# A scatter without waits among its own kind, a table cleared from DRAM, and loads issued earlier, in a two-layer graph network

## The chip, the core and the metric

The kernel runs on one core of one Trainium2 chip. A core has a matrix engine (PE, whose weight loads are listed apart as PEld), a vector engine (DVE), an activation engine (ACT), a general engine (POOL), a sequencer (SP) that here only issues transfers, and 16 DMA engines that all queues share. The metric is the device time of one execution in microseconds; the median of three runs is given. A profile is one further execution with the hardware profiler on; its span is the time from the first to the last instruction.

## What is computed

The input is x of 6250 nodes with 256 features and 100 000 edges, sorted by destination. Four layers follow each other, and each adds its result to x:

```python
x = x + gat(layernorm(x), edge_index, ...)      # 8 heads x 32, softmax over the edges of a node, relu
x = x + moe_top1(layernorm(x), ...)             # 32 experts, 256 -> 64 -> 256, relu
x = x + rgcn(layernorm(x), edge_weight, ...)    # 16 relations, weighted sum over edges
x = x + moe_top2(layernorm(x), ...)             # 8 experts, 256 -> 512 -> 256, gelu, layernorm
```

The first mixture of experts is the one that the change bears on:

```python
logits = xf @ router_w.T + router_b
idx = jnp.argmax(logits, axis=-1)
w1t = jnp.take(W1, idx, axis=0)
h = jnp.einsum('nd,ndh->nh', xf, w1t) + jnp.take(b1, idx, axis=0)
h = jax.nn.relu(h)
w2t = jnp.take(W2, idx, axis=0)
out = jnp.einsum('nh,nhd->nd', h, w2t) + jnp.take(b2, idx, axis=0)
out = jax.nn.relu(out)
```

So every node goes through one of 32 small networks, and the kernel sorts the nodes by expert so that a tile of 128 nodes needs one expert's weights.

## The kernel before

**Attention.** After a preparation (L224 to L312) and a pass over the nodes that writes a row of 272 floats for each to the DRAM table H_tab and the destinations' terms to ad_tab (L651), a loop of 98 rounds (L1117) takes 1024 edges each. A round's eight gathers (L444, POOL) fetch 128 rows of 1088 B each by index. PE forms sums by destination (L502, L518), and L557 picks each edge's destination term from `aw`, a small tile that `load_terms` (L476) reads from ad_tab over SP's queue two rounds ahead, into one of three buffers. `load_dst` reads destination numbers on ACT's queue, also two rounds ahead, into `db` with two buffers.

**Order.** The whole loop stands under `tc.manual_schedule()` (L1108): every engine executes its instructions in the order in which the Python code emits them. In each round, between the picks of one group and the sums of another, `fill` (L1134) emits some of the following layer's work, by fixed budgets of time for each kind.

**The second layer beside it.** Nodes are handled in three chunks of tiles of 128 nodes, (0,6), (6,22) and (22,49), so that a chunk can start when the attention sums of its nodes are done. For each chunk generators emit: `take` (residual and norm), `route` (expert of each node, count, slot in the sorted order), `experts`, and `products` (the 16 relation products of the third layer, written to T_tab). `route` ends with a loop over the chunk's tiles (L868): rows are loaded from x1_tab into `xs2`, which has four buffers, three tiles ahead (L859), and scattered to their slots of the DRAM table `x_sort` by an indirect DMA on POOL (L870). The three chunks share one x_sort. Each scatter writes the whole table as far as the tracking of dependences knows, so each waits for the one before it. `experts` then loads tiles of x_sort (`xs`, L928) and of the weight table `w_tab` (L922) on SP, transposes (L915), multiplies (L904, L892), adds into `ys` (L894, two buffers) and stores to y_sort (L935).

**The tables.** Slots of a chunk are padded to whole tiles for each expert, so unused slots have to hold zeros, and w_tab has padding as well. Once, in the first rounds, the generator `flow.consts` (L674) is stepped by `next(boot, None)` (L1133), one step a round. It clears w_tab whole from a tile of zeros in SBUF (L692), fills its parts (L694 to L697), and clears x_sort by 58 DMAs of one tile (L700), four in a round; then the relation weights `wr` are loaded (L705), two a round. `route` waits with its scatters (in the emission of code) until `self.ready` says that the clears are emitted.

**Afterwards.** A second block (L1145) emits what is left of the second layer. Then the third layer gathers rows of T_tab (L444 again, 784 gathers named `ts`), and the last layer follows (L1210 to L1345).

Of the kernel before, what the change touches and what calls it, by code (L numbers as in the profile page):

```python
# [14 lines left out]
ALU = mybir.AluOpType  # L15
AX = mybir.AxisListType
DVE = mybir.EngineType.DVE
SP = mybir.EngineType.SP
# [28 lines left out]
def gnn_ffn_kernel(  # L47
# [91 lines left out]
    ew_sb = const.tile([P, T, NG], F32, name="ew_sb")  # L139
    dst_f = const.tile([P, T, NG], F32, name="dst_f")  # L140

# [20 lines left out]
    B1C = W2C + D  # L162
    w_tab = dram.tile([E1, P, B1C + 4], F32, name="w_tab")
    x1_tab = dram.tile([N, 2 * D], F32, name="x1_tab")
    x2_tab = dram.tile([N, D], F32, name="x2_tab")

    class Chunk:


        def __init__(self, a, b, x_sort=None):  # L170
            self.a, self.b, self.nt = a, b, b - a
            self.xt = (min(N, b * P) - a * P + E1 * (P - 1)) // P
            self.x_sort, self.sorted, self.free, self.taken = x_sort, False, lambda: True, []
            if x_sort is None:
                self.x_sort = dram.tile([self.xt * P, 2 * D], F32, name=f"x_sort{a}_{b}")
            self.y_sort = dram.tile([self.xt * P, D], F32, name=f"y_sort{a}_{b}")

# [46 lines left out]
    with tc.tile_pool(name="prep", bufs=1) as prep, tc.tile_pool(name="prep_p", bufs=1, space=PSUM) as prep_p:  # L224
# [71 lines left out]
        nc.vector.scalar_tensor_tensor(i1f, nat["src"], float(NREL), nat["rel"], op0=ALU.mult, op1=ALU.add)  # L296
        for a, o in ((dgf, dst_f), (srf, src_i), (i1f, idx1), (nat["ew"], ew_sb)):
            for h in range(2):
                w = T // 2
                pt = prep_p.tile([P, w, NG], F32, name="pt", bufs=2)  # L300
                for t in range(w):
                    c = (h * w + t) * P
                    nc.tensor.transpose(pt[:, t, :], a[:, c : c + P], ident[:NG, :NG])
                if a is dgf:
                    nc.vector.tensor_tensor(
                        rlm[:, h * w : (h + 1) * w, :].rearrange("p (q u) g -> p q u g", u=QT),
                        pt.rearrange("p (q u) g -> p q u g", u=QT),
                        lo4[:, h * Q // 2 : (h + 1) * Q // 2, None, :].to_broadcast([P, Q // 2, QT, NG]), ALU.subtract)
                if h == 0:
# [94 lines left out]
    class Group:  # L404


        def __init__(self, pool, g, dynamic):
            self.g, self.pool, self.dynamic = g, pool, dynamic
            if not dynamic:
                self.idx0 = lambda t: src_i[:, t, g : g + 1]  # L410
                self.idx1 = lambda t: idx1[:, t, g : g + 1]
                self.w, self.rl = ew_sb[:, :, g], rlm[:, :, g]
                self.win = lambda i: win[:, i, g : g + 1]
                return
            ii = pool.tile([P, 2, T], I32, name="d_ii")
            fw = pool.tile([P, 2, T], F32, name="d_fw")
            for o, a in ((ii[:, 0], src_i), (ii[:, 1], idx1), (fw[:, 0], dst_f), (fw[:, 1], ew_sb)):
                nc.vector.tensor_copy(o.rearrange("p (t o) -> p t o", o=1), a[:, :, ds(g, 1)])
            self.di = pool.tile([P, T], I32, name="d_di")
            nc.vector.tensor_copy(self.di, fw[:, 0, :])  # L420
# [38 lines left out]
        def load_dst(self):  # L459

            n = GE if self.dynamic else QT * P
            self.db = self.pool.tile([P, n], I32, name="db", bufs=1 if self.dynamic else 2)
            if self.dynamic:
                nc.sync.dma_start(self.db, dst_rows[ds(self.g, 1), :].to_broadcast([P, GE]))
                return
            for q in range(Q):
                nc.scalar.dma_start(self.db[q * QW : (q + 1) * QW, :],
                                    bass.AP(tensor=dst.tensor, offset=dst.offset + self.g * GE + q * n,
                                            ap=[[0, QW], [1, n]]))
# [184 lines left out]
    class Flow:  # L654


        def __init__(self, es, bufs, psum_bufs):

            self.open, self.bufs = 0, 1
            self.ready = False  # L660
            enter = lambda name, **kw: es.enter_context(tc.tile_pool(name=name, **kw))
# [11 lines left out]

        def consts(self, zero):  # L674

# [15 lines left out]
            nc.vector.tensor_copy(self.rwT, pr[:, : KC * E1].rearrange("p (k e) -> p k e", k=KC))  # L691
            nc.sync.dma_start(w_tab.rearrange("e p w -> p e w"), zr[:, None, : B1C + 4].to_broadcast([P, E1, B1C + 4]))  # L692
            for k in range(KC):
                nc.sync.dma_start(w_tab[:, :, k * H1 : (k + 1) * H1], f1_w1[:, k * P : (k + 1) * P, :])  # L694
            nc.sync.dma_start(w_tab[:, :H1, W2C:B1C], f1_w2)
            nc.sync.dma_start(w_tab[:, H1, W2C:B1C], f1_b2)
            nc.sync.dma_start(w_tab[:, :H1, B1C], f1_b1)  # L697
            yield
            for c in range(zero.shape[0] // P):
                nc.sync.dma_start(zero[c * P : (c + 1) * P, :], zr)  # L700
                if c % 4 == 3:
                    yield
            self.ready = True
            for r in range(NREL):
                nc.sync.dma_start(self.wr[:, :, r, :], rel_w[r].rearrange("(k p) o -> p k o", p=P))  # L705
                if r % 2 == 1:
                    yield

# [49 lines left out]
        def route(self, ck):  # L758
# [93 lines left out]
            nc.vector.tensor_reduce(cnt, le, AX.X, ALU.add)  # L852
            while not (ck.free() and self.ready):
                yield None
# [13 lines left out]
            for j in range(ck.nt):  # L868
                r, xs2 = ahead.pop(0)
                nc.gpsimd.indirect_dma_start(  # L870
                    out=ck.x_sort[:, :], out_offset=bass.IndirectOffsetOnAxis(ap=ck.slot[:r, j : j + 1], axis=0),
                    in_=xs2[:r, :], in_offset=None)
                if j + 3 < ck.nt:
                    ahead.append(rows(j + 3))
                if j % 8 == 7:
                    yield 0, 0.1

        def experts(self, ck):
# [7 lines left out]
            for s in range(np_ + 5):  # L886
                if 4 <= s < np_ + 4:
# [3 lines left out]
                    for j in range(n):  # L891
                        nc.tensor.matmul(po[:, j * D : (j + 1) * D], lhsT=hid[:, j, :], rhs=lv["w"][j][: H1 + 1, W2C:B1C], start=True, stop=True)  # L892
                    ys = pool.tile([P, 2, D], F32, name="ys", bufs=2)
                    nc.vector.scalar_tensor_tensor(ys[:, :n, :], po[:, : n * D].rearrange("p (n d) -> p n d", n=n), 0.0,  # L894
# [23 lines left out]
                if 2 <= s < np_ + 2:  # L918
                    lv = live[s - 2]
                    for j in range(lv["n"]):  # L920
                        w = pool.tile([P, B1C + 4], F32, name="w", bufs=6)
                        nc.sync.dma_start(w, w_tab[ds(lv["e"][j], 1)].rearrange("o p w -> (o p) w"))  # L922
                        lv["w"].append(w)
                if s < np_:
                    c, n = pairs[s]
                    lv = live[s] = {"c": c, "n": n, "e": [], "w": []}
                    xs = lv["xs"] = pool.tile([P, 2, 2 * D], F32, name="xs", bufs=5)
                    nc.sync.dma_start(xs[:, :n, :], xs_rows[:, c : c + n, :])  # L928
                    for j in range(n):
# [119 lines left out]
    with ExitStack() as es_flow:  # L1049
# [5 lines left out]
        pi = es.enter_context(tc.tile_pool(name="ge_i", bufs=1, space=PSUM))  # L1055
        aws = [pr1.tile([P, Q, 2 * HEADS], F32, name=f"aw{i}") for i in range(3)]
        for a in aws:
# [113 lines left out]
    with tc.If(flag(2) > 0):  # L1171
# [3 lines left out]
        with ExitStack() as es_flow:  # L1175
            flow = Flow(es_flow, 1, 2)
            for _ in flow.consts(whole.x_sort):
                pass
# [199 lines left out]
```

## Time and profile before

| | us |
|---|---|
| runs | 3815.41, 3823.86, 3828.49 |
| median | 3823.86 |
| profiled execution | 3459.76 |
| its span | 3458.0 |
| PE busy | 2423.5 (70%) |
| POOL busy | 1713.0 (50%) |
| DVE busy | 1069.1 (31%) |
| ACT busy | 803.6 (23%) |

The profiled execution is 364 us shorter than the median of the runs. The mean granted clock of PE was 0.727 of full speed.

How to read the lines that follow. The page cuts the span into 40 equal slices of 86 us, and a digit gives an engine's busy tenths in a slice, 9 for 90% and more. A group of instructions is a line of code, an engine, an operation and its output and input, with the number of instructions, the busy time and the mean in ns of one, and after the bar the idle time ahead of them and what ended most of it. A line of waits gives an engine, what it was to do, whom it waited for, and the total us, the number of waits and the longest one. A line of the timeline begins with start and duration in us; the bracket at its end has the idle time ahead of the instruction and what released it. A line of a DMA queue gives packets, MB, and the share of the 16 engines' time that they took.

### The profile page before, as it was taken

Reading aid. Unit: us, or ns where it says so; the run is one execution under the profiler, and the core shown is the slowest. Engines: PE = TensorE matmul, PEld = TensorE weight load, DVE = VectorE, ACT = ScalarE, POOL = GpSimd, SP = SyncE. Lnnn points to the kernel's source line nnn. Section 1 sums busy time; section 2 is a strip of 40 time slices with the busy share of each in tenths; the row PEclk is TensorE's granted clock in tenths of the full one; section 3 lists DMA queues with packets and bytes.
Section 4 is the critical chain, followed back from the end, with each engine's and each line's share of the span. In section 5 each row is a group of like instructions: output and inputs, shape, how many; then the busy total and the mean of one; then the engine's idle time right before and its main releaser. Section 6 shows DMA issues by size and latency. Waiting matters only on the chain. (4 is left out here: it accounts for less than half of the span.)

```text
span 3458.0 us, 32167 instructions
## 1 busy us (share of the span) xinstructions
PE 2423.5 (70%) x8917; PEld 1186.0 (34%) x8918; DVE 1069.1 (31%) x2879; ACT 803.6 (23%) x1684; POOL 1713.0 (50%) x1736
## 2 busy tenths in 40 slices
PE   5334457791675987188999966666666666689997
PEld 4212235341453443054444421111111111166665
DVE  7324646562555653011000002121121211242222
ACT  2112223440333443033333310000000000012332
POOL 0447676774757771200000047777777777622222
PEclk9655576885676999589999975555555555569999
DMA  4697687675886774586444453333333333310000
GB/s 146 193 217 244 186 278 229 200 227 177 265 264 186 227 219 161 169 264 219 168 171 170 159 188 105 105 105 105 105 105 105 105 105 105 89 28 19 19 19 20
DMA packets 326688, 533.40 MB, mean 154 GB/s; under 512 B 84966, under 2 KB 182564, under 8 KB 326496
## 3 DMA queue, kind: packets, MB, share of 16 engines
q1 hardware_dynamic: 218060, 277.92, 24.4%
q0 software_dynamic: 83152, 233.62, 23.7%
q10 hardware_dynamic: 25284, 19.67, 1.9%
q8 instruction: 75, 1.23, 0.2%
q14 instruction: 117, 0.96, 0.1%
HBM read 342.80 MB, written 192.42 MB: 155 GB/s over the span
## 5 line engine op out<-in xcount | busy, mean ns | idle before, releaser
L444 POOL DMA_INDIRECT hs<-H_tab,src_i x784 | 765.7, 977 | 428.3 <-issue 212.0
L444 POOL DMA_INDIRECT ts<-T_tab,idx x784 | 743.7, 949 | 330.4 <-issue 238.5
L998 PE MATMUL pb<-wr,xTt 128*128 128x512 f32 (+1 forms) x1568 | 722.2, 617 | 18.6 <-ACT tr L1001 14.1
L502 PE MATMUL qagg<-ts,oh 128*32 128x256 f32 x1568 | 504.6, 630 | 327.7 <-DMA ts<-T_tab,idx 324.0
L998 PEld LDWEIGHTS pb<-wr,xTt 128*128 128x128 f32 (+1 forms) x1568 | 303.9, 198 | 387.8 <-issue 356.7
L502 PEld LDWEIGHTS qagg<-ts,oh 128*32 128x32 f32 x1568 | 90.2, 139 | 719.9 <-DMA ts<-T_tab,idx 640.4
L1001 ACT COPY tr<-pb 128x512 f32<-128x512 f32 (+1 forms) x392 | 228.4, 587 | 452.7 <-PE pb L998 344.1
L509 ACT COPY qs<-qagg 128x264 f32<-128x264 f32 (+1 forms) x196 | 73.9, 377 | 1117.0 <-PE qagg L502 1095.3
L454 DVE TENSOR_TENSOR oh<-iota,rlm 128x256 f32<-128x256 f32 x196 | 83.1, 425 | 799.2 <-PE qagg L502 793.5
L518 PE MATMUL agg<-qs,pl 128*128 128x264 f32 (+1 forms) x392 | 204.4, 619 | 146.2 <-DVE pl L511 81.9
L557 PE MATMUL pe<-aw,oT 128*128 128x64 f32 x392 | 86.4, 362 | 296.2 <-issue 140.0
L952 POOL DMA_INDIRECT yg<-y_sort,slot x49 | 47.1, 961 | 489.0 <-ACT xl L717 291.6
L579 DVE TENSOR_TENSOR hs<-hs,pe 128x2048 f32<-128x2048 f32 x98 | 223.2, 2277 | 0.0
L557 PEld LDWEIGHTS pe<-aw,oT 128*128 128x128 f32 x392 | 76.5, 267 | 339.6 <-issue 247.9
L1328 PE MATMUL ph<-xT,we 128*128 128x512 f32 (+1 forms) x416 | 177.4, 584 | 15.1 <-DMA we<-in_L_ffn_W_dram,ix 11.7
L518 PEld LDWEIGHTS agg<-qs,pl 128*128 128x128 f32 x392 | 91.2, 280 | 270.5 <-ACT qs L509 162.6
L1336 PE MATMUL po<-we,hid 128*128 128x256 f32 (+1 forms) x784 | 171.9, 379 | 0.5 <-DVE we L1314 0.3
L1336 PEld LDWEIGHTS po<-we,hid 128*128 128x128 f32 (+1 forms) x784 | 148.4, 190 | 26.8 <-issue 5.7
L502 PE MATMUL qagg<-hs,oh 128*32 128x264 f32 x1568 | 155.7, 533 | 0.0
L894 DVE SCALAR_TENSOR_TENSOR ys<-pb,xs 128x512 f32<-128x512 f32 (+1 forms) x72 | 49.2, 684 | 324.8 <-PE pb L892 180.0
L904 PE MATMUL pb<-xTe,w 128*64 128x128 f32 x568 | 99.6, 326 | 40.1 <-DMA w<-w_tab 35.3
L915 PE MATMUL pt<-ident,xs 128*128 128x128 f32 x284 | 58.7, 341 | 95.6 <-DMA xs<-x_sort 92.7
(278 smaller groups left out, 2303.7 us busy)
## 6 DMA issues: line engine op xcount, KB each, us to landing
T_tab<-tr SPq DMA_DIRECT2D x384, 256.0 KB
xs<-x_sort SPq DMA_DIRECT2D x70, 512.0 KB
w<-w_tab SPq DMA_DIRECT2D x142, 194.0 KB
y_sort<-ys SPq DMA_DIRECT2D x70, 256.0 KB
x_sort<-xs SPq DMA_DIRECT2D x58, 256.0 KB
db<-in_dst_dram ACTq DMA_DIRECT2D x392, 32.0 KB
hs<-H_tab,src_i POOLq DMA_INDIRECT x784
ts<-T_tab,idx POOLq DMA_INDIRECT x784
```

The source lines that it names most:

```text
L444: nc.gpsimd.indirect_dma_start(out=hs[:, t, :], out_offset=None, in_=table, in_offset=bass.IndirectOffsetOnAxis(ap=idx(t), axis=0))
L454: nc.vector.tensor_tensor(oh, iota[:, None, :n].to_broadcast([P, T, n]), column(self.rl), ALU.is_equal)
L502: nc.tensor.matmul(ps[q * QW : (q + 1) * QW, :width], lhsT=oh[:, t, :], rhs=vals[:, t, :width], start=u == 0, stop=u == QT - 1)
L509: nc.scalar.copy(qs, ps[:, :width])
L518: nc.tensor.matmul(ps[:, :width], lhsT=pl, rhs=qs, start=True, stop=True)
L557: nc.tensor.matmul(pq[:, u * w : (u + 1) * w], lhsT=oT[:, u, :], rhs=aw.rearrange("p q h -> p (q h)"), start=True, stop=True)
L579: nc.vector.tensor_tensor(hv, hv, pv.to_broadcast([P, T, HEADS, HD]), ALU.mult)
L904: nc.tensor.matmul(ph[:H1, j * P : (j + 1) * P], lhsT=lv["w"][j][:, k * H1 : (k + 1) * H1], rhs=xT[:, k, j * P : (j + 1) * P], start=k == ...
L998: nc.tensor.matmul(pr[:r, :], lhsT=xT[:, k, j * P : j * P + r], rhs=self.wr[:, k, q0 : q0 + 2, :], start=k == 0, stop=k == KC - 1)
L1001: nc.scalar.copy(o2, pr[:r, :])
L1328: nc.tensor.matmul(ph[:, :nn], lhsT=we1[:, i, k, c * P : (c + 1) * P], rhs=xT[:, k, :nn], start=k == 0, stop=k == KC - 1)
L1336: nc.tensor.matmul(po[:r, :], lhsT=hid[:, i, c, j * P : j * P + r], rhs=we2[:, i, c, :], start=i + c == 0, stop=i + c == NFC)
```

## The change

The scatters of one chunk are declared independent of each other, and the load of the sorted rows waits for all of them. x_sort is cleared two tiles at a time, one such DMA in a round, from a DRAM table of zeros, z_tab. w_tab has rows of 385 instead of 388 floats, is no longer cleared whole, and its parts are filled one in a round; only its padding is written with zeros. Scatters may be emitted as soon as the clears of as many tiles as the chunk needs have been emitted (`first` is the smallest of these numbers). Destination terms are loaded four rounds ahead into six buffers, destination numbers three rounds ahead into three. POOL is no longer among the engines whose order is that of the code: the scheduler orders it. `ys` has a third buffer. The copy dst_f, which only a fallback path read, is gone.

```diff
-    w_tab = dram.tile([E1, P, B1C + 4], F32, name="w_tab")
+    w_tab = dram.tile([E1, P, B1C + 1], F32, name="w_tab")
+    z_tab = dram.tile([P, 2 * D], F32, name="z_tab")
...
-            self.db = self.pool.tile([P, n], I32, name="db", bufs=1 if self.dynamic else 2)
+            self.db = self.pool.tile([P, n], I32, name="db", bufs=1 if self.dynamic else 3)
...
-        def consts(self, zero):
+        def consts(self, zero, first):
+            nt = zero.shape[0] // P
+
+            def clear(n):
+                n = min(n, nt - self.cleared)
+                if n:
+                    o = zero[self.cleared * P : (self.cleared + n) * P, :].rearrange("(c p) d -> c p d", p=P)
+                    nc.sync.dma_start(o, z_tab[None, :, :].to_broadcast([n, P, 2 * D]))
+                    self.cleared += n
...
-            nc.sync.dma_start(w_tab.rearrange("e p w -> p e w"), zr[:, None, : B1C + 4].to_broadcast([P, E1, B1C + 4]))
-            for k in range(KC):
-                nc.sync.dma_start(w_tab[:, :, k * H1 : (k + 1) * H1], f1_w1[:, k * P : (k + 1) * P, :])
-            nc.sync.dma_start(w_tab[:, :H1, W2C:B1C], f1_w2)
-            nc.sync.dma_start(w_tab[:, H1, W2C:B1C], f1_b2)
-            nc.sync.dma_start(w_tab[:, :H1, B1C], f1_b1)
-            yield
-            for c in range(zero.shape[0] // P):
-                nc.sync.dma_start(zero[c * P : (c + 1) * P, :], zr)
-                if c % 4 == 3:
-                    yield
-            self.ready = True
+            nc.sync.dma_start(z_tab, zr)
+            parts = [(w_tab[:, :, k * H1 : (k + 1) * H1], f1_w1[:, k * P : (k + 1) * P, :]) for k in range(KC)]
+            parts.append((w_tab[:, H1:, W2C:], z_tab[None, H1:, : D + 1].to_broadcast([E1, P - H1, D + 1])))
+            parts.append((w_tab[:, :H1, W2C:B1C], f1_w2))
+            parts.append((w_tab[:, H1, W2C:B1C], f1_b2))
+            parts.append((w_tab[:, :H1, B1C], f1_b1))
+            while self.cleared < first:
+                if parts:
+                    nc.sync.dma_start(*parts.pop(0))
+                clear(2)
+                yield
+            for o, i in parts:
+                nc.sync.dma_start(o, i)
             for r in range(NREL):
                 nc.sync.dma_start(self.wr[:, :, r, :], rel_w[r].rearrange("(k p) o -> p k o", p=P))
-                if r % 2 == 1:
-                    yield
+                clear(2)
+                yield
+            while self.cleared < nt:
+                clear(2)
+                yield
...
-            while not (ck.free() and self.ready):
+            while not (ck.free() and self.cleared >= ck.xt):
                 yield None
...
-                nc.gpsimd.indirect_dma_start(
+                ins = nc.gpsimd.indirect_dma_start(
                     out=ck.x_sort[:, :], out_offset=bass.IndirectOffsetOnAxis(ap=ck.slot[:r, j : j + 1], axis=0),
                     in_=xs2[:r, :], in_offset=None)
+
+                ck.put.append(ins.ins)
+                tc.declare_no_dep(ins.ins, group=ck.key, reason="no two nodes share a slot")
+                tc.add_to_no_dep_group(ck.key, ins.ins)
...
-                    ys = pool.tile([P, 2, D], F32, name="ys", bufs=2)
+                    ys = pool.tile([P, 2, D], F32, name="ys", bufs=3)
...
-                    nc.sync.dma_start(xs[:, :n, :], xs_rows[:, c : c + n, :])
+                    ins = nc.sync.dma_start(xs[:, :n, :], xs_rows[:, c : c + n, :])
+                    for put in ck.put:
+                        tc.add_manual_dep(ins.ins, put.name, mybir.DependencyInfo(
+                            mybir.DependencyClass.Sync, mybir.DependencyReason.DATA), reason="all rows are there")
...
-        aws = [pr1.tile([P, Q, 2 * HEADS], F32, name=f"aw{i}") for i in range(3)]
+        aws = [pr1.tile([P, Q, 2 * HEADS], F32, name=f"aw{i}") for i in range(6)]
...
-        with tc.manual_schedule():
-
-            boot = flow.consts(chunks[0].x_sort)
+        with tc.manual_schedule(engines={PE, DVE, ACT, SP}):
+
+            boot = flow.consts(chunks[0].x_sort, min(ck.xt for ck in chunks))
             groups = [Group(pg, g, False) for g in range(NG)]
-            for g in range(2):
-                groups[g].load_dst()
-                groups[g].load_terms(aws[g % 3])
+            for g in range(4):
+                if g < 3:
+                    groups[g].load_dst()
+                groups[g].load_terms(aws[g])
...
-                if g + 2 < NG:
-                    groups[g + 2].load_dst()
-                    groups[g + 2].load_terms(aws[(g + 2) % 3])
+                if g + 3 < NG:
+                    groups[g + 3].load_dst()
+                if g + 4 < NG:
+                    groups[g + 4].load_terms(aws[(g + 4) % 6])
...
-        with tc.manual_schedule():
+        with tc.manual_schedule(engines={PE, DVE, ACT, SP}):
             while takes or routes or runs or tails:
                 fill(4.0, 8.0, (1, 1, 1, 9))
```

More of the change, by code (lines that the diff above doesn't have):

```diff
@@ L16 @@
 AX = mybir.AxisListType
+PE = mybir.EngineType.PE
 DVE = mybir.EngineType.DVE
@@ L139, in gnn_ffn_kernel @@
     ew_sb = const.tile([P, T, NG], F32, name="ew_sb")
-    dst_f = const.tile([P, T, NG], F32, name="dst_f")
     rlm = const.tile([P, T, NG], F32, name="rlm")
@@ L175, in __init__ @@
                 self.x_sort = dram.tile([self.xt * P, 2 * D], F32, name=f"x_sort{a}_{b}")
+            self.key, self.put = f"put{a}_{b}", []
             self.y_sort = dram.tile([self.xt * P, D], F32, name=f"y_sort{a}_{b}")
@@ L296, in gnn_ffn_kernel @@
         nc.vector.scalar_tensor_tensor(i1f, nat["src"], float(NREL), nat["rel"], op0=ALU.mult, op1=ALU.add)
-        for a, o in ((dgf, dst_f), (srf, src_i), (i1f, idx1), (nat["ew"], ew_sb)):
+        for a, o in ((dgf, None), (srf, src_i), (i1f, idx1), (nat["ew"], ew_sb)):
             for h in range(2):
@@ L308, in gnn_ffn_kernel @@
                         lo4[:, h * Q // 2 : (h + 1) * Q // 2, None, :].to_broadcast([P, Q // 2, QT, NG]), ALU.subtract)
+                if o is None:
+                    continue
                 if h == 0:
@@ L416, in __init__ @@
             fw = pool.tile([P, 2, T], F32, name="d_fw")
-            for o, a in ((ii[:, 0], src_i), (ii[:, 1], idx1), (fw[:, 0], dst_f), (fw[:, 1], ew_sb)):
+            for o, a in ((ii[:, 0], src_i), (ii[:, 1], idx1), (fw[:, 1], ew_sb)):
                 nc.vector.tensor_copy(o.rearrange("p (t o) -> p t o", o=1), a[:, :, ds(g, 1)])
             self.di = pool.tile([P, T], I32, name="d_di")
-            nc.vector.tensor_copy(self.di, fw[:, 0, :])
+            nc.sync.dma_start(self.di, dst_rows[ds(g, 1), :].rearrange("g (t p) -> p (g t)", p=P))
+            nc.vector.tensor_copy(fw[:, 0, :], self.di)
             self.base = pool.tile([P, 1], F32, name="d_base")
@@ L659, in __init__ @@
             self.open, self.bufs = 0, 1
-            self.ready = False
+            self.cleared = 0
             enter = lambda name, **kw: es.enter_context(tc.tile_pool(name=name, **kw))
@@ L920, in experts @@
                     for j in range(lv["n"]):
-                        w = pool.tile([P, B1C + 4], F32, name="w", bufs=6)
+                        w = pool.tile([P, B1C + 1], F32, name="w", bufs=6)
                         nc.sync.dma_start(w, w_tab[ds(lv["e"][j], 1)].rearrange("o p w -> (o p) w"))
@@ L1176, in gnn_ffn_kernel @@
             flow = Flow(es_flow, 1, 2)
-            for _ in flow.consts(whole.x_sort):
+            for _ in flow.consts(whole.x_sort, whole.xt):
                 pass
```

## The prediction, made before the changed kernel had run

> **What bounds the kernel now.** I read the slices of the span first, then the waits, then the timeline at every POOL gap. The slices give busy tenths of 86 us each:
>
> ```profile
> PE   5334457791675987188999966666666666689997
> POOL 0447676774757771200000047777777777622222
> DMA  4697687675886774586444453333333333310000
> ```
>
> To slice 15 POOL's gathers of attention rows set the pace, 784 of them:
>
> ```profile
> L444 POOL DMA_INDIRECT hs<-H_tab,src_i x784 | 765.7, 977 | 428.3 <-issue 212.0
> q1 hardware_dynamic: 218060, 277.92, 24.4%
> x_sort<-xs SPq DMA_DIRECT2D x58, 256.0 KB
> ```
>
> A gather takes 0.98 us and 0.27 us of issue, so 1.25 us; an undisturbed round of eight takes 10.0 us (98 rounds, 114 to 1293 us). Then come routing and scatters of the last chunk (to 1454), its experts (1608), products (1990, PE), relational gathers (3100, POOL), the last FFN (3458, PE). The change touches 114 to 1608 only, so a shift there moves the end by as much. The waits (engine, line, releaser: total us, times, longest) that it aims at:
>
> ```profile
> POOL x_sort L870 <- DMA x_sort<-xs,slot: 102.1, 41, 3.7
> PE pt L915 <- DMA xs<-x_sort: 92.7, 2, 69.2
> PE pe L557 <- DMA aw<-ad_tab: 80.7, 7, 44.4
> DVE ys L894 <- DMA y_sort<-ys: 78.8, 14, 9.8
> ```
>
> The timeline places them (start, us, engine, line; in brackets the wait):
>
> ```profile
> 199.83 8.11 SPq L476 DMA_DIRECT2D aw<-ad_tab  x4
> 209.54 1.09 PE L557 MATMUL pe<-aw,oT 128*128 128x64 f32 x4 [44.44 <-DMA aw<-ad_tab]
> 212.93 1.01 POOL L444 DMA_INDIRECT hs<-H_tab,src_i  x1 [35.11 <-PE qagg L502]
> ...
> 416.34 1.00 POOL L870 DMA_INDIRECT x_sort<-xs,slot  x1 [0.30 <-issue]
> 439.35 1.09 PE L915 MATMUL pt<-ident,xs 128*128 128x128 f32 x4 [23.56 <-DMA xs<-x_sort]
> ...
> 785.92 0.99 POOL L870 DMA_INDIRECT x_sort<-xs,slot  x1 [0.30 <-DVE hs L579]
> 847.20 0.96 POOL L870 DMA_INDIRECT x_sort<-xs,slot  x1 [2.02 <-DMA x_sort<-xs,slot]
> 887.11 1.06 PE L915 MATMUL pt<-ident,xs 128*128 128x128 f32 x4
> ...
> 1358.23 0.99 POOL L870 DMA_INDIRECT x_sort<-xs,slot  x1 [39.15 <-DVE le L850]
> 1450.38 1.56 POOL L870 DMA_INDIRECT x_sort<-xs,slot  x1 [3.50 <-issue]
> ```
>
> Read there: destination terms queued behind the table clears stop PE for 44 us and POOL for 35; six scatters of chunk 1 precede its first experts matmul at 439.35; 16 scatters of chunk 2 hold POOL from 785.9 to 848.5; 27 scatters of chunk 3 run while PE, the weight loads and almost everything else stand still.
>
> **What the Trainium skill says.** "DMA: Bandwidth & Descriptors" has three things. Its section "Why a DMA increments its semaphore by 16 and not by 1" says that a DMA is spread over the largest number of engines, at most 16, that divides the slowest dimension of both patterns, and the rules for authors there warn that a leading broadcast of c copies confines the DMA to c engines. No DMA of the trace before shows this at such a size. "Specifications" puts one engine at some 27 GiB/s (29 GB/s); the trace has 22.9: in 162 to 174 us the hardware queue moved 2.71 MB in 61.7% of 16 engines × 12 us. "Anatomy of one DMA" has about 2 us of fixed completion latency; the trace agrees, with 2.0 us of wait after each 0.96 us scatter.
>
> **The change part by part.**
>
> *Clears.* Before, 58 clears of 256 KB left SBUF with 128 partitions outermost. Now 29 clears of 512 KB go from DRAM to DRAM, and the pattern in the program is 2 × 4 × 16384: its outermost size is the two copies. By the rule each uses two engines, 262,144 B on each. At the trace's 22.9 GB/s that is 11.5 us; at the page's 29, an estimate, 9.0. The descriptors are larger than the trace's, so I take the middle, 10.3. One clear is issued in a round, and a round's gathers also put 8 × 8 × 1088 B = 69.6 KB on each engine, 3.0 us at 23.3 GB/s (software queue, same window). 13.3 us don't fit in 10.0: in the clearing rounds two engines become the bound, and the gathers, whose rows lie on all 16, wait for these two.
>
> When does chunk 1 start? SP issues 24 or 25 clears before the rows of its scatters, and the first scatters wait for the clears' completions. Work on the two engines from 156 us (the first clear): 25 × 10.3 = 257; gathers to group 28, behind which POOL's new order puts the scatters (232 instead of 208 gathers; some 39 are done), 193 × 0.374 = 72; weight table 36 (30 us before, 183 to 213, and a sixth for its zeros); small loads 15. Sum: 536. The gathers left, six scatters of at least 1.25 us, their landing and the row load add 20: L915 at 556 instead of 439.35, **+117**. With 9.0 us a clear and half the other terms beside idle engines it is 501, +62; with 11.5 and larger terms 618, +179. Were the clears free, L915 would stand at 424: the start stall of 35 us goes, 24 gathers come ahead (+30), scatters lose their waits (about −10): −15. PE's order is fixed and has attention work behind L915, so what L915 loses the later rounds lose, POOL too, by buffers.
>
> *Destination terms four rounds ahead, weight table in parts.* Both remove the wait at 209.54, counted above. The clear of 6.2 MB becomes 2.1 MB of zeros. The aw loads now share SP with one clear a round rather than four; six buffers let SP run at most three rounds ahead of PE, and an SP that waits for a DMA lane behind two clears (2 × 10.3) holds aw, rows and weight loads behind it. Four rounds, 40 us, cover 21. If the clears were slower than a round by more than this, PE would meet L557 late: rival C.
>
> *Scatters of chunk 2.* They are now strewn among gathers 472 to 504. The last stands 56 operations after 785.9: 56 × 1.254 = 70, so 856, and L915 at 862 instead of 887.1: **−25** (bounds −15, −32: the next hindrance is PE itself, which stalled some 25 us for work between 953 and 1056).
>
> *Scatters of chunk 3.* (1450.38 − 1358.23)/26 = 3.54 us apart. Without the wait each is held by POOL (1.25 us), the bytes (256 KB read, 256 KB written; 512 KB at the 383 GB/s of 162 to 174 us is 1.4), or its source rows, which have four buffers: scatter 1.0, landing 2.0 and the next row load, 3.4 if it takes what the xs load does from issue to use (1458.60 to 1461.97), make a loop of 6.4, a quarter of it 1.6. I take 1.7: 26 × (3.54 − 1.7) = **−48** (bounds −35 at 2.2, −58 at 1.3). Late next: the row load, then the xs load, which now waits for all 27.
>
> *Third ys buffer.* In chunk 3's experts DVE waited 33 us for y_sort stores, with DMA at 0.79 there: **−5** (0 to −15); the cover is PE, busy 122 of 154 us. *dst_f copies*: one ACT copy and one DVE copy in preparation, 0.5 us each: −1. *Weight rows of 1540 instead of 1552 B*: 0 (±3).
>
> Sum: +117 − 25 − 48 − 5 − 1 = +38. The first term's error leans down, since part of a slower gather phase is taken out of waits that the later rounds have anyway; I take **+30**. The profiled execution was 3459.76 us (span 3458.0), 364 below the median of 3823.86; nothing in the trace accounts for that, and the change is carried over unscaled: **3854**, a profile of about 3490.
>
> **The rivals.**
>
> A, faster: the clears spread over 16 engines, or their cost lies beside POOL's pace. 512 KB at 366 GB/s is 1.4 us a round, and the windows of 280 to 320 have DMA 0.78 busy, so it fits. Then −15 − 25 − 48 − 5 − 1 = −94: **3730**. For it: all other terms of the change are gains whose waits stand in the trace. Against it: the access pattern.
>
> B, no change: two engines, but at the page's rate and with the gathers mostly beside: +62 + 15 (waits absorbed less) − 79 = −2, give or take 10: **3822**.
>
> C, slower, and more than forecast: SP's queue decides. Clears slower than 22.9 GB/s, as they both read and write DRAM; from 13 us a clear SP falls more than four rounds behind, so that aw (L476) and the row loads come late to PE in rounds 10 to 29. Then 25 × 2.7 = 68 more: +98, **3922**.
>
> D: the scatters still wait for each other, by shared DMA lanes or row buffers. Chunks 2 and 3 gain nothing: the forecast turns to +103 (3927), and A to −21 (3803). For it: row buffers stay four. Against it: the loop above.
>
> **How the numbers follow.** A difference counts above 0.3%, 11 us, about what a measurement of this kernel can tell from none. Chances: forecast case 0.42 (its own range 3810 to 3925, from the bounds of the clears: +62 to +179 less 79, cut at the upper end where the slower gather phase hides part), A 0.30, B 0.12, C 0.10, D 0.06. Of the forecast case 0.34 ends slower, 0.03 the same, 0.05 faster; A is faster; B splits 0.04 faster, 0.05 same, 0.03 slower; C is slower; D is 0.04 slower, 0.02 faster. Faster 0.41, same 0.08, slower 0.51. The range 3720 to 3930 takes in A and most of C.
>
> **What would show it.** The clears' durations: about 10 us each (two engines) or 1 to 2 (sixteen). Rounds between 160 and 500 us at 13 us or at 10. First L915 near 556, or 424. A POOL wait at the first scatter of chunk 1, released by a clear. L557 waits below 5 us at the start. Chunk 3's scatters 1.7 us apart instead of 3.54. Chunk 2's L915 25 us earlier counted from chunk 1's. I am wrong first of all if the clears are not confined to two engines.

## The result, and the profile after

The changed kernel took 3953.75 us (median of 3952.68 to 3960.24), the kernel before 3822.02 beside it: a ratio of 1.0348, 95% interval 1.0327 to 1.037. It is slower by 132 us, where +30 was forecast and 3930 was the upper end.

The slices of the changed kernel's page (busy tenths, 99 us each) show POOL and DMA low in slices 5 to 7, about 400 to 690 us:

```profile
PE   6213221466726747684899993222222222258998
POOL 0445342456665556511000005666666666623222
DMA  4574334665667746547844445333333333311000
```

Its group of attention gathers has the same busy time as before and more idle time (809.1 us), most of the addition in waits for PE; its waits name what was late:

```profile
L449 POOL DMA_INDIRECT hs<-H_tab,src_i x784 | 764.4, 975 | 809.1 <-PE qagg L507 319.5
...
PE pe L562 <- DMA aw<-ad_tab: 131.3, 9, 28.0
POOL x_sort L890 <- DMA xs<-x_tab: 63.7, 20, 35.0
```

A second profile of the kernel before, of 3827 us and so nearer to the runs than the first one, has 608.0 us of idle time there and these lines:

```profile
POOL hs L444 <- PE qagg L502: 137.4, 21, 31.4
POOL x_sort L870 <- DMA x_sort<-xs,slot: 101.4, 41, 3.7
PE pe L557 <- DMA aw<-ad_tab: 63.9, 2, 39.2
```

So the scatters' waits for each other are gone, and some of them became waits for their rows. The waits for destination terms, which the change was to remove, doubled.

The profile shown ahead of the prediction came from an execution of 3459.76 us, while the runs had 3824: the kernel before takes 3809 to 3857 us in some sets of runs and 3441 to 3464 in others, and each kernel's ratio is to the kernel before of its own set. The table has one pair of profiles at each of the two levels; the first is called the pair at 3456 below. Starts in us, from the timelines of POOL and PE:

| | before (first profile) | changed (second profile) | diff. | before again | changed | diff. |
|---|---|---|---|---|---|---|
| attention round 8 | 233 | 215 | −18 | 248 | 226 | −22 |
| round 18 | 336 | 373 | +37 | 364 | 399 | +35 |
| round 29 | 464 | 646 | +182 | 523 | 687 | +164 |
| first experts matmul, chunk 1 | 439 | 621 | +182 | 494 | 663 | +169 |
| round 36 | 548 | 772 | +224 | 622 | 815 | +193 |
| first experts matmul, chunk 2 | 887 | 1119 | +232 | 1038 | 1208 | +171 |
| first scatter, chunk 3 | 1358 | 1595 | +237 | 1598 | 1767 | +168 |
| last scatter, chunk 3 | 1450 | 1652 | +202 | 1690 | 1825 | +134 |
| first gather of the third layer | 2026 | 2220 | +194 | 2263 | 2397 | +134 |
| span | 3458 | 3651 | +193 | 3825 | 3959 | +133 |

All of the net loss arises between rounds 8 and 36, while x_sort is cleared; the later stages together give some back.

**Where in these rounds.** The starts of every eighth gather give the rounds. Changed kernel above, below it the changed kernel with the clear spread over all engines (first experiment), rounds 8 to 31, us:

```
changed 32.6 18.9 24.5 14.2 15.7 12.6 13.7 14.7 12.3 14.0 59.4 14.1 11.6 10.2 46.0 13.6 10.1 13.0 11.6 11.5 86.4 23.6 12.8 27.8
spread  17.0 19.5 17.5 11.8 11.7 10.2 13.2 12.4 10.0 13.4 19.7 12.5 11.9 10.2 13.0 12.3 11.6 11.7 11.8 15.3 33.6 14.1 12.9 12.5
```

Most rounds are at most a few us longer (rounds 10 and 29 by 7 and 9); five (8, 18, 22, 28 and 31) are 15 to 53 us longer. Summed, rounds 8 to 17 are 37 us longer than with spread clears, rounds 18 to 27 71 us, round 28 alone 53, rounds 29 to 35 25. Round 18 in the changed kernel's timeline, the store of chunk 1's node tiles and the next load, both on SP:

```profile
420.80 0.62 SPq L689 DMA_DIRECT2D x_sort<-z_tab  x1
421.54 0.41 SPq L114 DMA_DIRECT2D x_tab<-xr  x1
431.54 0.64 SPq L689 DMA_DIRECT2D x_sort<-z_tab  x1
441.91 0.76 DVE L764 TENSOR_TENSOR xr<-ring,den 128x256 f32<-128x256 f32 x2 [42.07 <-DMA x_tab<-xr]
441.96 0.41 SPq L114 DMA_DIRECT2D xr<-in_x_dram  x1
452.35 0.69 DVE L770 SCALAR_TENSOR_TENSOR xr<-xr 128x512 f32<-128x512 f32 x1 [8.46 <-DMA xr<-in_x_dram]
455.34 1.09 PE L562 MATMUL pe<-aw,oT 128*128 128x64 f32 x4 [54.62 <-DVE hs L584]
458.73 1.01 POOL L449 DMA_INDIRECT hs<-H_tab,src_i  x1 [49.66 <-PE qagg L507]
```

Read it upwards. POOL waits 50 us for PE, PE 55 for DVE, and DVE stands at L764, which overwrites the buffer `xr` and has to wait for its store to x1_tab (`x_tab` in the profile). SP came to that store only at 421.5, behind two clears issued at 411.7 and 420.8, and it landed 20 us later. In the first experiment it is issued at 361.75 and DVE's wait for stores from 160 to 640 us is 2.0 us instead of 70.0. SP's own waits from 160 to 500 us say what it was doing, in the changed kernel:

```profile
SPq L481 <- DMA x_sort<-z_tab: 77.5, 10, 8.9
SPq L481 <- DMA db<-in_dst_dram: 60.2, 4, 39.3
```

Destination terms (L481) don't read x_sort: these are waits for a completion lane, a semaphore that tells of a transfer's landing and that several transfers use in turn. In this trace clears, destination terms and the destination numbers of ACT's queue share eight of them. The wait of 39.3 us comes right after the stop of round 18: SP has issued the clears of the next rounds, then it stands until ACT's load has landed (446 to 486 us), and from 462 to 498 us no clear moves. After the stop of round 22 the same wait takes 50.5 us.

The DMA view of 431.6 to 438.9 us has a clear nearly by itself:

```profile
DMA packets 53, 0.40 MB, mean 54 GB/s; under 512 B 46, under 2 KB 46, under 8 KB 47
q1 hardware_dynamic: 53, 0.40, 12.8%
```

12.8% of 16 engines is two engines. That is what the Trainium skill's "DMA: Bandwidth & Descriptors" says in "Why a DMA increments its semaphore by 16 and not by 1": an outermost size of two leaves two engines. Each carries 27 GB/s here, so a clear of 524,288 B takes 9.7 us by itself. In the trace it is four pieces of 64 KB on each engine, 2.42 us a piece.

### The profile page after: what moved, and what is told of

It is laid out like the page before. It is cut to its first block, busy times and chain, and to the rows that moved or that the text cites. A ratio compares the mean times of both kernels' runs of the same rounds, so it can differ in the third digit from the quotient of the medians.

```text
span 3958.5 us, 31967 instructions
## 1 busy us (share of the span) xinstructions
PE 2136.9 (54%) x8917; PEld 1166.2 (29%) x8918; DVE 1068.1 (27%) x2881; ACT 798.5 (20%) x1683; POOL 1717.0 (43%) x1736
## 5 line engine op out<-in xcount | busy, mean ns | idle before, releaser
L449 POOL DMA_INDIRECT hs<-H_tab,src_i x784 | 764.4, 975 | 809.1 <-PE qagg L507 319.5
L1025 PE MATMUL pb<-wr,xTt 128*128 128x512 f32 (+1 forms) x1568 | 732.6, 623 | 53.8 <-issue 27.7
L507 PE MATMUL qagg<-ts,oh 128*32 128x256 f32 x1568 | 191.6, 616 | 20.4 <-DMA ts<-T_tab,idx 19.8
L531 DVE SCALAR_TENSOR_TENSOR ring<-agg,win,ring 128x264 f32 x196 | 96.6, 493 | 250.6 <-PE agg L523 169.7
L531 DVE SCALAR_TENSOR_TENSOR acc<-agg,win,acc 128x256 f32 x196 | 94.2, 481 | 140.4 <-issue 60.4
L928 PEld LDWEIGHTS pb<-xTe,w 128*64 128x64 f32 x568 | 77.2, 168 | 154.3 <-issue 124.5
```

Of the source, the lines that this page charges most:

```text
L449: nc.gpsimd.indirect_dma_start(out=hs[:, t, :], out_offset=None, in_=table, in_offset=bass.IndirectOffsetOnAxis(ap=idx(t), axis=0))
L507: nc.tensor.matmul(ps[q * QW : (q + 1) * QW, :width], lhsT=oh[:, t, :], rhs=vals[:, t, :width], start=u == 0, stop=u == QT - 1)
L531: nc.vector.scalar_tensor_tensor(a, ps[:, :width], self.win(w), a, op0=ALU.mult, op1=ALU.add)
L928: nc.tensor.matmul(ph[:H1, j * P : (j + 1) * P], lhsT=lv["w"][j][:, k * H1 : (k + 1) * H1], rhs=xT[:, k, j * P : (j + 1) * P], start=k == ...
L1025: nc.tensor.matmul(pr[:r, :], lhsT=xT[:, k, j * P : j * P + r], rhs=self.wr[:, k, q0 : q0 + 2, :], start=k == 0, stop=k == KC - 1)
```

## The experiments

**The kernel before again**, to place the 364 us.

> The kernel before, unchanged, to have a profile of it beside those of the other runs. If the profile shown before (3460 us, 364 below the median) was of a rare execution, this one comes out at about 3820, and the stages show where the 360 us lie. If profiling itself makes this program shorter, about 3460 again.

Measured: 3826.93 us. Most rounds take about 11.7 instead of 10.0 us, and the third layer's 784 gathers 1109 instead of 982; the page's busy time of POOL is the same (1714.9 and 1713.0). What holds the gathers there is not settled.

**Clears with the partitions outermost.**

```diff
-  o = zero[...].rearrange("(c p) d -> c p d", p=P)
-  nc.sync.dma_start(o, z_tab[None, :, :].to_broadcast([n, P, 2 * D]))
+  o = zero[...].rearrange("(c p) d -> p c d", p=P)
+  nc.sync.dma_start(o, z_tab[:, None, :].to_broadcast([P, n, 2 * D]))
```

> The changed kernel with one edit: the clear's pattern has the 128 partitions outermost instead of the two copies, same bytes, same DMAs. Theory 1, the clears are confined to two engines and everything on SP's queue stands behind them there: the first experts matmul comes near 424 to 450 us instead of 663, and the time falls to about 3730 (3710 to 3770), below the kernel before. Theory 2, one clear a round on SP's queue with shared completion lanes is what holds SP, however it is spread: 3900 to 3955, the matmul after 600. Theory 3, the new order of POOL or the wait of the row load for all scatters costs the time: 3900 or more with early clears, and the loss after 1000 us.

Measured: 3774.4 us, ratio 0.9882 (0.9854 to 0.991); first experts matmul at 504.6. Same bytes, same DMAs, same places in the queue: theories 2 and 3 fall. The time is 44 us above the 3730 that I expected, and the first experts matmul, expected at 424 to 450, still 11 us later than in the kernel before, so the part about free clears was too good as well.

**The same, with the scatters chained again** (the two lines that declare them independent are taken out).

> As the run with the 128 partitions outermost, and the scatters of a chunk wait for each other again. If independent scatters are worth what I worked out (25 us in chunk 2, 48 in chunk 3), it is some 60 to 75 us slower than that run, about 3800; if the scatters are held by their row loads in any case, the same within 15 us.

Measured: 3826.51 us, 1.0012 (0.9997 to 1.0027), 52 us more than with independent scatters, where 60 to 75 were expected. The rest of the change, its clears spread, is then worth nothing that shows.

**Clears on four engines.**

```diff
-  .rearrange("(c p) d -> c p d", p=P)
+  .rearrange("(c p) d -> c p d", p=P // 2)
-  z_tab[None, :, :].to_broadcast([n, P, 2 * D])
+  z_tab[None, : P // 2, :].to_broadcast([2 * n, P // 2, 2 * D])
```

> The changed kernel, the same clears cut so that the outermost size is four. Theory 1: the bytes on each of the engines halve, 131 KB a clear, about 4 us beside 3 of gathers in a round of 10, so most of the loss goes: 3740 to 3800, first experts matmul 430 to 500. Theory 2 and 3: about 3950 as with two.

Measured: 3864.65 us in a single run, first experts matmul at 583.0, between what the theories expected. A clear nearly by itself, 388.5 to 393.35 us, uses four engines at the same 27 GB/s each:

```profile
DMA packets 149, 0.53 MB, mean 109 GB/s; under 512 B 141, under 2 KB 141, under 8 KB 141
q1 hardware_dynamic: 147, 0.53, 26.7%
```

Sixteen, four and two engines give 504.6, 583.0 and 663.2 us for the matmul, and 3774, 3865 and 3954 in all. At 27 GB/s an engine a clear takes 1.2 (an estimate), 4.8 and 9.7 us; the 29 clears are then 104 and 247 us longer than with sixteen, against 90 and 179 measured. Much of the added time shows, but not everywhere. Rounds 11 to 17 take 11.8 us on average with sixteen engines and with four, and 13.9 with two: on four engines the clears are hidden in the ordinary rounds, as I had expected. What is lost with four is lost mostly in rounds 18, 22 and 28, which take 37.6, 35.2 and 66.6 us, against 19.7, 13.0 and 33.6 with sixteen. The DVE's waits for x1 stores are 2.0, 47.0 and 70.0 us in the three.

The "about 4 us" in this expectation and the "8 us" in the next two fit 66 GB/s for a clear on two engines. The DMA view of 420 to 500 us shows that figure in its slices of 2 us, because there a packet's bytes count whole where it starts, two pieces of 64 KB in most slices. The pieces' own durations give the 54 GB/s and 9.7 us above.

**Clears on ACT's queue**, still on two engines (`nc.scalar.dma_start` for `nc.sync.dma_start` in the clear).

> The changed kernel with its clears (two copies outermost, so two engines and the same bytes on them) issued from ACT's queue instead of SP's. Theory A, order in the queue: a load or store of SP that something waits for stands in the same two rings behind two or three clears, 8 us each[...]: the long rounds 18, 22 and 28 (59.5, 46.0 and 86.4 us in the changed kernel, 19.7, 13.1 and 33.6 with spread clears) shrink by more than half, first experts matmul 505 to 570, time 3775 to 3860. Theory B, work of the two engines: the bytes are the same, so it stays at 3920 to 3960 with the matmul after 620. The destination numbers on ACT's queue now stand behind clears, three rounds ahead; if that isn't enough, ACT waits show it.

Measured: 3888.52 us, 1.0113 (1.0076 to 1.0149); first experts matmul 590.1; rounds 18, 22 and 28 take 12.6, 17.0 and 52.0 us; DVE's wait for stores is 14.0, and PE's wait for destination terms between 160 and 640 us, 106.1 in the changed kernel, is gone (ACT has 35.2 us of it). Theory A holds for the long rounds, though round 28 shrinks by less than half and rounds 19 and 23 are 7 to 8 us longer: with equal bytes on two engines, taking the clears out of SP's queue gives back 73 of the 159 us by the first experts matmul. The time misses A's range by 29 us (the kernel before took 21 us more in this set than in that of the first experiment). ACT now waits 99.9 us for destination numbers behind the clears (12.7 in the changed kernel), and rounds 4 to 6 take 23.2, 32.8 and 17.5 instead of 10.3, 12.5 and 10.9 us. Counted from round 8 on, the way to the first experts matmul takes 322 us, against 437 in the changed kernel and 278 with spread clears: there 115 of 159 us are given back. What the remainder is, work of the two engines or waits on ACT's queue, this run can't say.

**No clears around the node tiles.**

```diff
-  next(boot, None)
+  if g not in (14, 15, 16, 19, 20, 23):
+      next(boot, None)
```

> The changed kernel, clears on two engines, but the generator isn't stepped in rounds 14 to 16, 19, 20 and 23, in which the node tiles of chunk 1 are stored and loaded; 20 clears instead of 25 come before its scatters, the others after. Theory A: the rounds with 59.5 and 46.0 us fall to 20 to 30 and 13 to 25, first experts matmul 575 to 605 (one round of emission later), time 3880 to 3910, less what the clears moved behind it cost there. Theory B: five clears of 8 us fewer, spread over all rounds: the long rounds stay above 40, the matmul 620 to 640.

Measured: 3969.83 us in a single run, beside 3842.94 for the kernel before. Rounds 18 and 22 fall to 35.2 and 27.9, less than A expected and more than B; the first experts matmul stands at 627.9, in B's range, and the time is 60 us above A's. Rounds 32 to 37, where clears now meet the experts' loads, take 35.2, 27.6, 26.9, 24.7, 24.2 and 25.9 us, against 13.2, 20.3, 14.8, 15.9, 14.5 and 15.2 in the changed kernel. Moving the clears along SP's queue moved the loss and didn't lessen it; between A and B this run alone doesn't decide.

**Spread clears and early router weights** (the loads of bias and router weights and the zero tile stand ahead of the first destination terms).

> Clears with 128 partitions outermost, and the loads of bias and router weights issued ahead of the first destination terms. In the run with spread clears PE stands 30.3 us at L706 for router weights queued on SP behind 20 loads of destination terms; with the load first, the round of 32.3 us falls to 12 to 18, and if nothing else is late there the time falls by 10 to 20 us, to about 3757. If the next wait (destination terms of round 1, weight table) takes its place, within 5 us of 3774.

Measured: 3779.35 us where the kernel before had 3842.94: 0.984 (0.9811 to 0.987). Round 3 falls from 32.3 to 16.2 us, as expected, and the first experts matmul comes 13.6 us earlier. The interval overlaps that of the run without it, so a gain in the whole time isn't shown. In the first experiment the wait was this:

```profile
PE pb L706 <- DMA xs<-in_L_ffn_router_w_dram: 30.3, 1, 30.3
```

Eight more loads of destination terms stand on SP ahead of these weights, because terms are loaded two rounds earlier. The kernel before has this wait too, though: it is 9.1 us there and 16.1 in the changed kernel in the pair at 3456, 22.4 and 29.3 in the other pair. The edit that removes the 35 us stall adds 7 us here.

**Six row buffers** (`xs2` six instead of four, five tiles ahead; `xs` four instead of five).

> As the one before, and six row buffers instead of four for the scatters, loaded five tiles ahead (paid for by four instead of five buffers for the sorted rows). If row loads hold the scatters, the 27 of chunk 3 come down from about 58 us to 35 to 45, time 10 to 20 us below the one before; if the bytes hold them, no change. The missing buffer may cost up to 10 us in the experts.

Measured: 3764.72 us, 0.9787 (0.9757 to 0.9817). First and last scatter of chunk 3, in the changed kernel and then in this one:

```profile
1766.74 0.99 POOL L890 DMA_INDIRECT x_sort<-xs,slot  x1 [39.26 <-DVE le L870]
1824.52 1.56 POOL L890 DMA_INDIRECT x_sort<-xs,slot  x1 [4.88 <-issue]
```

```profile
1576.98 0.99 POOL L890 DMA_INDIRECT x_sort<-xs,slot  x1 [39.17 <-DMA xs<-x_tab]
1622.05 1.57 POOL L890 DMA_INDIRECT x_sort<-xs,slot  x1 [2.74 <-issue]
```

57.8 us become 45.1, 2.22 us a scatter become 1.73; the run before this one, which differs in the buffers alone, has 56.1. So row loads held them. The whole time is 15 us lower, as expected, with intervals that overlap barely.

**Terms two rounds ahead, clears spread** (three and two buffers as before).

> Clears with 128 partitions outermost, and the destination terms and numbers again two rounds ahead (three and two buffers), so that only the longer lead is taken out. If the lead is what removes the second stall of the start (31 us for POOL in the kernel before), the time rises by 10 to 30 us over the run with spread clears, to a ratio of 0.992 to 0.996; if the 20 loads that stand ahead of the router weights cost as much as the lead saves, the ratio stays at 0.985 to 0.991 and PE's wait at L706 falls from 30 to below 24 us.

Measured: 3440.06 us, 0.996 (0.9941 to 0.9978), in a set in which the kernel before took 3452. PE's wait for router weights is 9.6 us, against 16.1 with the longer lead (changed kernel, second profile). Round 8 starts at 220, in the kernel before at 233 and with the longer lead at 215 (changed kernel), so 13 of the 18 us are had without the longer lead. The ratio lies in the range for a lead that matters, but because the kernel before is at another level here than beside the first experiment, the two ratios can't settle the lead's worth; this was inconclusive.

**The scatters alone**, in the kernel before (independent scatters, the row load's waits, POOL's free order).

> The kernel before, with the independent scatters, the row load's wait for all of them and POOL's free order, nothing else. Chaining them again in the run with spread clears gave back 1.3% of the time, 52 us by the profiles' ends. If this part is worth the same on its own, the ratio is 0.984 to 0.990; if part of it depends on the other edits (early clears, earlier terms), 0.991 to 0.998. Without the clears in one row on SP there is no reason for a loss: above 1.003 would say that POOL's new order costs something.

Measured: 3414.13 us, 0.9894 (0.9867 to 0.9922) with the kernel before at 3452; within what was expected. By the profiles (spans 3410.8 and 3458.0) it gains 47 us: the 27 scatters of chunk 3 take 54.2 instead of 92.2. In chunk 2 nothing remains. The first gathers of rounds 56, 62 and 70 start at 766, 881 and 964 in the kernel before, at 767, 847 and 960 here: from round 56 to 62 34 us are gained, and all but some 5 are given back by round 70. The waits of this run between rounds 62 and 70, of POOL, PE and DVE:

```profile
POOL hs L446 <- PE qagg L504: 29.3, 7, 14.2
```

```profile
PE pe L559 <- DVE hs L581: 47.8, 6, 33.7
```

```profile
DVE xr L752 <- DMA xr<-in_x_dram: 27.2, 1, 27.2
```

POOL waits for PE, PE for DVE, and DVE for the next load of node tiles. That load was issued at 863.45 only: SP had been held by row loads, each of which waits for the scatter that frees its buffer, and the scatters now stand among gathers, the last one at 855.1 instead of 847.2. SP's waits between 800 and 880 us:

```profile
SPq L114 <- DMA x_sort<-xs,slot: 47.2, 12, 15.4
```

The changed kernel has the same wait of DVE in its chunk 2, 28.3 us.

This version and the one before it ran in one set, and their times don't overlap (3412.58 to 3420.74 and 3423.62 to 3445.38). So the rest of the change, with spread clears and without the longer lead, costs some 26 us here beside the scatters alone. By the profiles it is 13 us ahead at round 8, 8 behind at round 29 and 22 behind at round 56.

**The changed kernel and the six-buffer version again**, in one set.

> The changed kernel again. The last two runs' kernel before took 3452 us, like the profile shown at first, and 3822 to 3843 in the runs ahead of them. If the loss is work and order on two DMA engines it does not depend on that: some 130 us in either case (ratio 1.033 to 1.041). If it came only from the slower of the two cases, the ratio is below 1.02 when the kernel before takes 3452 here, and 1.03 to 1.04 when it takes 3820.

> The fastest version so far (clears with 128 partitions outermost, early router loads, six row buffers) beside the changed kernel: ratio to the kernel before 0.976 to 0.984 as in its first run, so 5 to 6% below the changed kernel. When the kernel before takes 3452, its stalls are a larger share and POOL's pace is nearer to 10 us a round: 0.970 to 0.985.

Measured, with the kernel before at 3456.34: changed 3658.29, ratio 1.0581 (1.0563 to 1.0599), +202 us, more than the 130 I expected; six buffers 3427.69, 0.991 (0.9892 to 0.9927), less gain than expected. The loss doesn't come from the longer executions; it is larger without them. That these have waits of their own which hide part of it would fit, but isn't shown. Spread clears with six row buffers were ahead of the kernel before in both sets in which they ran, the scatters alone in their one, with the same gain there (0.9894) as six buffers in this set (0.991).

## Why the prediction was right in sign and wrong in size

**Right.** The clears are confined to two engines, and the price of one holds: 10.3 predicted, 9.7 us by itself, and the 25 clears ahead of chunk 1's scatters took 254 us on each engine in the pair at 3456, where 257 were counted. There is luck in it: 10.3 was the middle between a rate of other packets and the skill's figure for one engine. Ordinary rounds in which clears are issued take about 13.9 us (rounds 11 to 17 of the changed kernel; 13.3 predicted), and that they fall to 11.8 with four engines fits two engines as the bound. But what arrives late in them is the destination terms, for which PE waits 9 to 11 us in five of these seven rounds, rather than the gathers. The scatters of chunk 3 without their chain gain 34 to 36 us; the later stages only shift; the sum is a loss.

**Wrong: the clears' term, +117.** It was a sum of work on two engines, taken as busy without a gap from 156 to 536 us, and 20 us more; the first experts matmul stood at 621 and 663, +182 and +169. What failed is that premise. In the pair at 3456 the clears begin at 181.2, 25 us late, since SP first stands 20.3 us for a completion lane that a load of ACT's queue holds. From there to the first scatter (605.2) no clear moves in 163 us, where the sum had 123 for all other work: 40 us more. Together that is the 65 us by which the term was too small. The two longest gaps, 30 and 39 us, follow the stops of rounds 18 and 22: SP stood 36.2 and 43.2 us for such a lane there.

The text named the lane and SP's queue, but it compared four rounds of lead (40 us) with a delay of 21, and took the terms as covered. They weren't: PE waited 151.8 us for them (131.3 in the other pair), where below 5 at the start was the sign to look for. And it overlooked the other things on SP's queue: the store and load of node tiles, on which DVE waits in order, with DVE the picks of PE, with PE POOL. The experiments with sixteen and four engines and with ACT's queue show the two parts, the work of few engines in the ordinary rounds and the order of the queue in the long ones; how much each costs alone isn't separated. Rival C had the mechanism (SP's queue decides), but only for clears slower than 13 us, and priced at 68.

The lower end of the term, 501 and +62, isn't what its words give: 156 + 25 × 9.0 + half of 123 + 20 is 463, +23. The range of the forecast and rival B rest on the +62.

**Wrong: clears behind the first scatters, priced at nothing.** 24 or 25 of 29 clears were counted. The others meet the first weight and row loads of the experts: round 29 to round 36 takes 126 instead of 84 us, +42 (+29 in the other pair, 128 for 99; with spread clears it is 103 there).

**Wrong: chunk 2, −25.** Rounds 56 to 70, in which these scatters lie, take 197 us instead of 199 in the pair at 3456 that the term was worked out for, and 213 instead of 231 in the other: there some of it came. The scatters alone moved that experts matmul by −1.3 us (887.1 to 885.8). "The next hindrance is PE itself" was not what came: strewing the scatters keeps SP behind their row buffers, and the node-tile load behind those stops DVE. The stall went from POOL to SP's queue.

**Mis-sized: chunk 3, −48.** −36 and −34 measured, at the edge of the bounds (−35): 2.2 us a scatter, held by row loads. The 2.0 us of wait after each scatter, from which the loop took the landing, was among the shortest; the mean in the first profile was 2.5 us (102.1 us in 41 waits). With six buffers it is 1.73, the value I took.

**The start, 35 us.** Of it 18 to 22 us were gained. The router weights' wait took 7 us, a step that I did not follow although every load that was moved ahead of them stood in the diff; where the rest went is open.

**Third ys buffer, −5.** From the experts' start of chunk 3 to the third layer the pair at 3456 gives 564 and 557 us, −7 for it and all that lies there.

In the pair in which the prediction's own profile is one half: +182 (clears and start) +42 and 13 more until chunk 3 (+237 at its first scatter), −36, −7 and −1 after that, together +193, the difference of the spans. With +117, 0, −25, −48, −5 and −1 it had been +38. The four large terms erred to the same side, and the text leaned the sum down to +30 as well.

## What to carry to other kernels

Before a transfer is moved from SBUF to a DRAM-to-DRAM copy, look at the outermost size of its access pattern: two here cost 179 us against 128 with the same bytes. Price a long transfer not only by its work but also by what stands behind it in its queue and who stops for that; a lead for one kind of load doesn't cover the others on the same queue. Where a stall is spread out or removed, follow the buffers that it frees: the queue that refills them may carry the stall on.

## What the runs showed of the hardware

One DMA engine moved 27 GB/s in these DRAM-to-DRAM copies with contiguous pieces of 64 KB, whether two or four worked at a copy; in the kernel before it was 22.9 over mixed packets. The store that was issued behind two such copies on the same queue landed after 20 us. Independent scatters of 128 rows were 2.2 us apart with four row buffers, 1.73 with six, and 3.5 when each waited for the last. The same program took about 3822 to 3843 us in some sets of runs and 3452 to 3456 in others; the difference lies in both gather stages (about 11.7 against 10.0 us a round, 1109 against 982 us for 784 gathers) with equal busy time of POOL, and the changed kernel's loss was 132 us in the one and 202 in the other. Each of the four sets of experiments ran on another chip, 6 and 3 at the longer level, 15 and 11 at the shorter; whether the chip decides was not tested.
